# Cross attention with two levels of Strassen-Winograd products: VectorE's sums interleaved, three products moved to fresh PSUM banks, and product 5 in blocks in every batch but the first

## The chip, the cores and the metric

The kernel runs on one NeuronCore of one Trainium2 chip. The metric is the device time of one execution in microseconds (us); the time before is the median of three runs. A NeuronCore has four engines with instruction queues of their own that matter here: TensorE (PE in the profile), which multiplies matrices into PSUM banks, VectorE (DVE), ScalarE (ACT) and GpSimd (POOL). SyncE (SP) issues DMAs, and so does POOL. Each queue runs in order; engines wait for one another through semaphores.

## The reference

Eight batches of 512 channels by 1024 positions; everything is float32.

```python
B, C1, C2, N = (8, 512, 512, 1024)
q = jnp.einsum('bcn,dc->bnd', x1, Wq) + bq            # d = 64
k = jnp.einsum('bcn,dc->bdn', x2, Wk) + bk[:, None]
v = jnp.einsum('bcn,dc->bdn', x2, Wv) + bv[:, None]
attn = jax.nn.softmax(jnp.einsum('bnd,bdm->bnm', q, k), axis=2)
attn_out = jnp.einsum('bcm,bnm->bcn', v, attn)
return attn_out + x1
```

## The kernel before

**Stages.** The kernel reorders the output as Wv (x2 exp(scores)) / sum, plus bias and x1. Per batch there are four stages on PE: queries and keys (`project`, L173), scores (`scores`, L212), y = x2 times the exponentials e (512 by 1024, contracted over 1024 positions), and o = Wv times y. The scores are transposed, so that e has the position that is summed over on the partitions: `e[0]` and `e[1]` are the left and right half of the columns (h = 0, 1), each with two groups of four tiles of 128 positions.

**Seven products.** Both y and o are 2 by 2 block products done with seven multiplications in place of eight (Strassen's method in Winograd's form). `MULT` (L355) lists the seven: left operand, right operand, PSUM bank, and whether the product opens its bank. Left operands S1 to S4 and right operands T1 to T4 are sums of blocks. A "bank" here is a pair, `a0` and `a1` or `c0` and `c1`, one for each 128 rows. A result that belongs to several outputs stays in its bank while further products are added to it, with a copy taken in between: ScalarE copies bank a after product 1 (u1), after 6 (u6) and after 5 (u5). In the names of the code: y11 = product 2 + u1, U3 = (products 1 + 6) + product 7, y22 = U3 + product 5, y21 = U3 and product 4, and T3 of the next level, y22 - y12, is product 7 and product 3.

**Products in blocks.** A product can itself be done with seven smaller ones (`inner_product`, L438): 128 by 256 results, two tiles deep. `inner_left` (L412) forms four 128x256 sums of the left operand, `inner_right` (L421) one 128x1024 and two 128x512 sums of the right operand, all on VectorE. Two half banks from the pool "sc" (two buffers, used in turn), `chain` and `third`, take the partial results. `multiply_seeded` (L459) opens a fresh bank: ScalarE copies the chain into parts of it (after inner products 1, 6, 5 and 4), further inner products are added there, and `complete` (L483) adds the third part on VectorE. `multiply_onto` (L489) instead adds to a bank that is in use and evicts the chain to a tile d in SBUF, which VectorE then completes (L516) and adds. Before, `multiply_seeded` serves products 1, 2, 7 and 3, `multiply_onto` serves 4 (`multiply_4`, L520, with another sum at L524) and, in batches 1 to 5, product 5 (`multiply_5`, L526, with two sums at L531). In batch 0 and in batches 6 and 7 product 5 is plain (`first(5)`), as product 6 is everywhere.

**Order.** All instructions are put in order by hand (`manual_schedule`, L987); `period` (L764) writes one batch and, between its products, work of the next batches: `n` is the next batch, `nn` and `nnn` the ones after (None past the end), `five` is true in batches 1 to 5. `hooks` of a product are calls that are made after one of its inner products, such as an exponential on ScalarE. `scores_0` (L790) makes the scores of the next batch's half 0 (one of the four in bank c), the queries of the batch after, and the running maximum over tiles (`fold`, L242; `highest`, L254, has POOL reduce over partitions). `lower` (L290) subtracts the maximum, `exponential` (L295) follows. The scores of half 1 come after product 3, the third of them in bank a. The sums of the exponentials (`total`, L260; `invert`, L269; `spread`, L275) go through POOL, three small DMAs and VectorE; `scale_y` (L544) multiplies y by the inverse.

**Sums off VectorE.** T4 is made from a ScalarE copy and two accumulating DMAs on POOL's queue (`sum_t4`, L315), T3 by a ScalarE negation and two such DMAs (`sum_t3`, L326), in batches 1 to 6. In batch 7 VectorE makes T3 (`sum_e`, L337).

## Time and profile before

| | |
|---|---|
| median of three runs | 682.66 us |
| lowest and highest | 682.51 and 682.8 us |
| span of the profiled execution (its own run isn't among the three) | 680.8 us |
| PE busy | 672.1 us (99%) |
| VectorE busy | 615.2 us (90%) |
| ScalarE busy | 336.9 us (49%) |
| GpSimd busy | 218.5 us (32%) |
| chain that ended last: PE, VectorE, DMA | 84%, 6%, 5% |
| granted PE clock | 0.9 or more of full speed in every fortieth of the span |

The span runs from the first to the last instruction of the program on the core, so it leaves out what comes before and after. A row of a timeline has the start from the span's beginning, the length, engine, line, operation, written tile and read tiles, shape, the number of merged instructions, and in brackets the idle time before it with what ended it. A row of waits has the sum, the number and the longest. Matmuls overlap: the next one starts while the one before still shows as busy, so a product's price is the distance between two starts. In float32 each matmul of the code shows as two. The batches follow one another without a gap; the first product of a batch starts at 120.46 (batch 1), 204.21, 286.25, 368.24, 450.42, 532.41 and 608.83 us (batch 7).

### The profile page before, as it was taken

The numbers are of one execution on the slowest core, as the hardware profiler recorded it, in microseconds if no ns is written. First come the engines' busy times: TensorE is split into PE (matmuls) and PEld (weight loads), VectorE is DVE, ScalarE is ACT, GpSimd is POOL, SyncE is SP. The second block draws the span as 40 slices with busy tenths as digits, with TensorE's granted clock in tenths as the row PEclk, the third lists the DMA queues.
The fourth block names the chain that finished last, engine by engine and source line by source line (L and its number), as shares of the span: only waits on it lengthen the run. The fifth ranks groups of instructions, "written<-read, shape, count | busy, mean of one in ns | idle before, by whom it ended". The sixth has DMA issues, their size and how long they took to land.

```text
span 680.8 us, 7209 instructions
## 1 busy us (share of the span) xinstructions
PE 672.1 (99%) x2420; PEld 397.9 (58%) x2420; DVE 615.2 (90%) x763; ACT 336.9 (49%) x564; POOL 218.5 (32%) x182
## 2 busy tenths in 40 slices
PE   8999999999999999999999999999999999999997
PEld 5333554757547565566656576464854747556763
DVE  1999998899999999999999998999989979999884
ACT  2734266365554564544644637446475356553320
POOL 0124215251153502643125421344213451154100
PEclk9999999999999999999999999999999999999999
DMA  9656658967798759969499693996947985489503
GB/s 300 271 191 241 155 212 139 240 138 246 180 249 221 154 202 253 214 185 245 123 297 199 174 264 116 280 212 160 277 89 174 222 194 110 92 146 268 144 13 110
DMA packets 50772, 131.09 MB, mean 193 GB/s; under 512 B 5552, under 2 KB 7856, under 8 KB 50736
## 3 DMA queue, kind: packets, MB, share of 16 engines
q0 software_dynamic: 22464, 54.60, 44.7%
q1 hardware_dynamic: 27984, 75.64, 30.8%
q10 hardware_dynamic: 288, 0.39, 0.2%
q8 instruction: 19, 0.31, 0.2%
q14 instruction: 17, 0.14, 0.1%
HBM read 87.30 MB, written 16.81 MB: 153 GB/s over the span
## 4 chain that ended last, share of the span: by engine, by line
PE 84%; DVE 6%; DMA 5%; issue 2%; ACT 1%; SPq 1%; POOL 1%; DVEq 0%; POOLq 0%; ACTq 0%
PE ps_ya L380 11%; PE ps_oa L380 11%; PE ps_yc L442 8%; PE ps_oc L380 7%; PE ps_ya L442 6%; PE ps_s L228 5%; PE ps_o L400 4%; PE ps_o L380 4%; PE ps_k L181 3%; PE ps_q L181 3%; PE ps_i4chain L442 3%; PE ps_i3chain L442 3%; PE ps_i7chain L442 2%; PE ps_i1chain L442 2%; PE ps_i2chain L442 2%
## 5 line engine op out<-in xcount | busy, mean ns | idle before, releaser
L263 POOL PARTITION_ALL_REDUCE den<-sum x16 | 52.6, 3285 | 97.4 <-DVE few L271 60.3
L258 POOL PARTITION_ALL_REDUCE top<-max x16 | 37.6, 2352 | 126.3 <-DVE max L252 75.7
L380 PE MATMUL ps_ya<-eT,aS 128*128 128x512 f32 x176 | 77.5, 594 | 0.0
L293 DVE TENSOR_TENSOR e<-e,top 128x1024 f32<-128x1024 f32 x60 | 69.9, 1218 | 0.0
L620 POOL DMA_DIRECT2D sum<-e x21 | 32.1, 1530 | 108.7 <-ACT sum L625 42.0
L297 ACT ACTIVATE e<-e 128x1024 f32<-128x1024 f32 x60 | 61.8, 1058 | 4.7 <-DVE e L293 4.0
L380 PE MATMUL ps_oa<-yT,w_S 128*128 128x512 f32 x128 | 57.5, 592 | 0.0
L380 PE MATMUL ps_oc<-yT,w 128*128 128x512 f32 x128 | 57.4, 592 | 0.0
L380 PEld LDWEIGHTS ps_ya<-eT,aS 128*128 128x128 f32 x176 | 33.2, 190 | 40.1 <-issue 37.9
L237 ACT COPY e<-ps_s 128x1024 f32<-128x1024 f32 x46 | 45.6, 1032 | 9.0 <-PE ps_s L228 8.8
L228 PE MATMUL ps_s<-q,k 64*128 64x512 f32 x188 | 47.9, 608 | 0.9 <-ACT q L647 0.8
L380 PEld LDWEIGHTS ps_oa<-yT,w_S 128*128 128x128 f32 x128 | 24.3, 190 | 30.6 <-issue 30.6
L380 PEld LDWEIGHTS ps_oc<-yT,w 128*128 128x128 f32 x128 | 24.3, 190 | 30.6 <-issue 29.2
L248 DVE TENSOR_TENSOR max<-max,e 128x1024 f32<-128x1024 f32 x30 | 36.7, 1225 | 2.2
L391 ACT COPY uo<-ps_oa 128x512 f32<-128x512 f32 x32 | 18.7, 586 | 34.9 <-PE ps_oa L380 34.9
L391 ACT COPY uy<-ps_ya 128x512 f32<-128x512 f32 x24 | 13.9, 588 | 36.8 <-PE ps_ya L380 36.8
L228 PEld LDWEIGHTS ps_s<-q,k 64*128 64x128 f32 x188 | 17.1, 186 | 24.5 <-issue 18.0
L479 ACT COPY ps_ya<-ps_i1chain 128x256 f32<-128x256 f32 x28 | 10.0, 357 | 42.2 <-PE ps_i1chain L442 38.7
L547 DVE TENSOR_TENSOR y<-y,den 128x1024 f32<-128x1024 f32 x24 | 29.3, 1221 | 0.3
L418 DVE TENSOR_TENSOR aI<-a 128x256 f32<-128x256 f32 x58 | 29.4, 547 | 0.0
L380 PE MATMUL ps_oa<-y,w_S 128*128 128x512 f32 (+1 forms) x68 | 28.8, 567 | 0.0
L400 PE MATMUL ps_o<-y,w 128*128 128x512 f32 x64 | 28.8, 592 | 0.0
(202 smaller groups left out, 1539.0 us busy)
## 6 DMA issues: line engine op xcount, KB each, us to landing
x_in_x_dram<-in_x_dram SPq DMA_DIRECT2D x60, 512.0 KB, 7.6
a<-in_x2T_dram SPq DMA_DIRECT2D x32, 512.0 KB, 10.1
sum<-e POOLq DMA_DIRECT2D x21, 512.0 KB, 10.1
aS<-in_x2T_dram POOLq DMA_DIRECT2D x14, 512.0 KB, 8.9
uo<-in_x_dram POOLq DMA_DIRECT2D x14, 512.0 KB, 9.9
r<-in_x_dram POOLq DMA_DIRECT2D x14, 512.0 KB, 12.2
out_dram<-r SPq DMA_DIRECT2D x14, 512.0 KB, 6.5
eT<-eT POOLq DMA_DIRECT2D x14, 512.0 KB, 10.1
```

Of the source, the lines that this page charges most:

```text
L181: nc.tensor.matmul(ps[r, :], w_sb[:, c, :], s.x[:, c, ts(h, H)], start=(c == 0), stop=(c == CT - 1),)
L228: nc.tensor.matmul(ps[g], s.k[r, ts(i, P)], s.q[r, ts(h, H)], start=True, stop=True)
L237: nc.scalar.copy(e[:, :, i, :], whole)
L248: nc.vector.tensor_tensor(f, e[:, :, 0, :] if i == 1 else f, e[:, :, i, :], op)
L258: nc.gpsimd.partition_all_reduce(s.top[h], s.mx[h][:, 0, :], P, ReduceOp.max)
L263: nc.gpsimd.partition_all_reduce(s.den[h], s.mx[h][:, 0, :], P, ReduceOp.add)
L293: nc.vector.tensor_tensor(e, e, top, ALU.subtract)
L297: nc.scalar.activation(e, e, AF.Exp)
L380: nc.tensor.matmul(ps[:, n], left[ka][:, k, ts(j, P)], right[kb][:, k, n], start=opens and k == 0, stop=i in (2, 3, 4) and k == n_k - 1, s ...
L391: nc.scalar.copy(s.tmp[i][:, j, :], ps)
L400: nc.tensor.matmul(ps, w["11"][:, k, ts(j, P)], s.y["11"][:, k, :], start=k == 0, stop=False, skip_group_check=True)
L442: nc.tensor.matmul(ps, s.inner[i][ka][:, k, :], s.inner[i, "t"][kb][:, k, :], start=opens and k == 0, stop=z in (2, 3, 4) and k == MH // 2 ...
```

## The change

- `weave` takes several streams of VectorE sums and issues them in turn, one from each. `left_stream` and `right_stream` are `inner_left` and `inner_right` as streams, `folds` and `lowers` are streams of these steps. Woven are: the folds of the sums of half 1 with product 7's left sums, the left and right sums of products 5 and 4, product 7's right sums with product 3's left ones, product 3's right sums with one lowering, and the next batch's right sums for product 1 with its left sums for product 2. From batch 1 on T1 is made for both pairs of tiles before T2.
- Product 5 is made by `multiply_seeded` in a fresh bank a in batches 1 to 7, so also in blocks in batches 6 and 7.
- Product 3 goes to a fresh bank c, product 4 to a fresh bank c (batch 7: bank a), from batch 1 on. ScalarE's copies of product 7 move ahead of product 3 and behind its second inner product. `join_67` adds u6 and that copy once; y22 is bank a + the sum, y21 bank c (batch 7: a) + the sum. `multiply_seeded` takes its second half bank only after the second inner product.
- Batch 7: T3 comes from ScalarE and DMAs as in the other batches, the total of half 1 and the inverse of half 0 are made later, and the sum T1 of y moves behind y21.

Batch 0 keeps its order and its product 4.

```diff
 
+    def folds(s, h, kind, op):
+
+        for i in range(1, MH):
+            fold(s, h, i, kind, op)
+            yield
+
     def fold_halves(s, h, op):
...
 
+    def lowers(s, h, of, to):
+        for i in range(of, to):
+            lower(s, h, i)
+            yield
+
     def exponential(s, h, i):
...
 
-    def sum_e(s, *ks, of=(0, 2)):
-        for i in of:
-            part = {n: v[:, i : i + 2, :] for n, v in s.t.items()}
-            for k in ks:
-                right_sums(part, k)
+    def sum_e(s, *ks):
+        order = [(k, i) for i in (0, 2) for k in ks]
+        for k, i in order if s.b == 0 else sorted(order):
+            right_sums({n: v[:, i : i + 2, :] for n, v in s.t.items()}, k)
 
...
     )
-    def inner_left(s, i, x, tag):
+    def weave(*streams):
+
+        streams = list(streams)
+        while streams:
+            for stream in list(streams):
+                if next(stream, "end") == "end":
+                    streams.remove(stream)
+
+    def left_stream(s, i, x, tag):
 
...
         sums = sb.tile([P, 4, MH // 2, P], F32, tag=tag, name=f"aI{i}_{s.b}")
+        s.inner[i] = v
         for z, (k, x, y, op) in enumerate(LEFT):
...
             nc.vector.tensor_tensor(v[k], v[x], v[y], op)
-        s.inner[i] = v
+            yield
 
-    def inner_right(s, i, x, *tags):
+    def inner_left(s, i, x, tag):
+        weave(left_stream(s, i, x, tag))
 
-        v = {
-            f"{q + 1}{r + 1}": x[:, ts(q, MH // 2), ts(r, H // 2)] for q in range(2) for r in range(2)
-        }
+    def right_stream(s, i, x, *tags):
+
+        half = x.shape[1] // 2
+        v = {f"{q + 1}{r + 1}": x[:, ts(q, half), ts(r, H // 2)] for q in range(2) for r in range(2)}
         last = 4 // len(tags)
-        shape = [P, last, MH // 2, H // 2]
+        shape = [P, last, half, H // 2]
         sums = [sb.tile(shape, F32, tag=t, name=f"eI{i}{t}_{s.b}") for t in tags]
...
         )
+        s.inner[i, "t"] = v | {"T1": both[:, 0], "T3": both[:, 1], "T2": t2, "T4": t4}
+        yield
         nc.vector.tensor_tensor(t2, both[:, 0], v["22"], ALU.subtract)
+        yield
         nc.vector.tensor_tensor(t4, v["21"], t2, ALU.add)
-        s.inner[i, "t"] = v | {"T1": both[:, 0], "T3": both[:, 1], "T2": t2, "T4": t4}
+        yield
+
+    def inner_right(s, i, x, *tags):
+        weave(right_stream(s, i, x, *tags))
 
...
 
-    def multiply_seeded(s, i, v_tag, hooks={}):
+    def multiply_seeded(s, i, v_tag, hooks={}, bank=None):
 
-        bank = MULT[i][2]
-        b0, b1 = (
-            ps_a.tile([P, H], F32, tag=f"{bank}{j}", name=f"ps_y{bank}{j}_{s.b}_{i}") for j in range(2)
-        )
-        s.bank[bank, 0], s.bank[bank, 1] = b0, b1
+        bank = bank or MULT[i][2]
+
+        def fresh(j):
+            s.bank[bank, j] = ps = ps_a.tile(
+                [P, H], F32, tag=f"{bank}{j}", name=f"ps_y{bank}{j}_{s.b}_{i}"
+            )
+            return ps
+
+        b0 = fresh(0)
         chain, third = inner_parts(s, i)
         v = sb.tile([P, 2, H], F32, tag=v_tag, name=f"v{i}_{s.b}")[:, 0, left]
-        for z, ps, opens, out, of in (
-            (1, chain, True, b0[:, left], chain),
-            (7, third, True, v, third),
-            (6, chain, False, b1[:, left], chain),
-            (2, b0[:, left], False, None, None),
-            (5, chain, False, b0[:, right], chain),
-            (4, b1[:, left], False, b1[:, right], chain),
-            (3, b0[:, right], False, None, None),
-        ):
+        def step(z, ps, opens, out=None, of=None):
             inner_product(s, i, z, ps, opens)
...
 
+        step(1, chain, True, b0[:, left], chain)
+        step(7, third, True, v, third)
+        b1 = fresh(1)
+        step(6, chain, False, b1[:, left], chain)
+        step(2, b0[:, left], False)
+        step(5, chain, False, b0[:, right], chain)
+        step(4, b1[:, left], False, b1[:, right], chain)
+        step(3, b0[:, right], False)
+
         def complete():
...
 
-        d, complete = multiply_onto(s, 4, "u5" if s.b < B - 1 else "a21", "r", hooks)
+        d, complete = multiply_onto(s, 4, "u5", "r", hooks)
         complete()
...
 
-    def multiply_5(s, hooks):
-
-        d, complete = multiply_onto(s, 5, "u5", "r", hooks)
-        complete()
-        for j in range(2):
-            nc.vector.tensor_tensor(d[:, j, :], s.bank["a", j], d[:, j, :], ALU.add)
-        s.tmp[5] = d
+    def join_67(s):
+        nc.vector.tensor_tensor(s.tmp[6], s.tmp[6], s.tmp[7], ALU.add)
 
...
         for j in range(2):
-            nc.vector.tensor_tensor(y[:, j, :], s.bank["a", j], s.tmp[7][:, j, :], ALU.add)
+            nc.vector.tensor_tensor(
+                y[:, j, :], s.bank["c" if s.b else "a", j], s.tmp[7][:, j, :], ALU.add
+            )
 
...
         bank, add = RESULT[k]
+        if s.b and k == "22" or s.b == B - 1 and k == "21":
+            bank, add = "a", 6
         s.y[k] = y = sb.tile([P, 2, H], F32, tag=f"y{k}", name=f"y{k}_{s.b}")
...
             complete_1()
-            for i in range(1, MH):
-                fold(s, 1, i, "sum", ALU.add)
-            total(s, 1)
-            invert(s, 0)
+            sums_5 = left_stream(s, 5, s.a["S1"], "i2"), right_stream(s, 5, s.t["T1"], "y21", "u1")
+            if n:
+                weave(folds(s, 1, "sum", ALU.add), left_stream(s, 7, s.a["S3"], "yT4"))
+                total(s, 1)
+                invert(s, 0)
+            else:
+                weave(folds(s, 1, "sum", ALU.add), left_stream(s, 7, s.a["S3"], "yT4"))
+                weave(*sums_5)
             complete_2 = multiply_seeded(
...
             )
-            if n:
-                sum_t3(s, 0)
-                sum_t3(s, 2)
+            sum_t3(s, 0)
+            sum_t3(s, 2)
+            if n is None:
+                total(s, 1)
             complete_2()
             evict_y(s, "11")
-            if n is None:
-                sum_e(s, "T3")
             sum_t4(s)
             first(6)
-            inner_left(s, 7, s.a["S3"], "yT4")
-            if five:
-                inner_left(s, 5, s.a["S1"], "i2")
-                inner_right(s, 5, s.t["T1"], "y21", "u1")
-            sum_a(s, "S4")
             if n:
+                weave(*sums_5)
+            if n:
+                sum_a(s, "S4")
                 evict_q = scores_0()
-            spread(s, 0)
-            shares(s, 1)
-            inner_right(s, 7, s.t["T3"], "yT1", "yT2")
-            inner_left(s, 3, s.a["S4"], "aI3")
-            if five:
-                multiply_5(s, {6: evict_q})
+                spread(s, 0)
+                shares(s, 1)
+            if n:
+                weave(right_stream(s, 7, s.t["T3"], "yT1", "yT2"), left_stream(s, 3, s.a["S4"], "aI3"))
             else:
-                first(5)
-            inner_right(s, 3, s.t["22"], "eT1")
+                sum_a(s, "S4")
+                weave(right_stream(s, 7, s.t["T3"], "yT1", "yT2"), left_stream(s, 3, s.a["S4"], "aI3"))
+                invert(s, 0)
+                spread(s, 0)
+            complete_5 = multiply_seeded(
+                s, 5, "r", {6: evict_q} if five else {}, "a"
+            )
+            complete_5()
+            if n is None:
+                shares(s, 1)
             if n:
-                lower(n, 0, 0)
+                weave(right_stream(s, 3, s.t["22"], "eT1"), lowers(n, 0, 0, 1))
+            else:
+                inner_right(s, 3, s.t["22"], "eT1")
             complete_7 = multiply_seeded(s, 7, "y12")
             complete_7()
-            evict_y(s, "22")
+            hooks = {7: lambda: copy_7(s, 1)}
             if n:
-                for i in range(1, MH):
-                    lower(n, 0, i)
-            else:
+                hooks |= {6: lambda: exponential(n, 0, 0), 4: lambda: exponential(n, 0, 1)}
+            copy_7(s, 0)
+            if n:
+                lower(n, 0, 1)
+            complete_3 = multiply_seeded(s, 3, "r", hooks, "c")
+            if n is None:
                 inner_left(s, 4, s.a["22"], "a12")
+            join_67(s)
+            evict_y(s, "22")
+            if n is None:
                 inner_right(s, 4, s.t["T4"], "eT2")
-
-            hooks = {2: lambda: copy_7(s, 0), 5: lambda: copy_7(s, 1)}
             if n:
-                hooks |= {6: lambda: exponential(n, 0, 0), 4: lambda: exponential(n, 0, 1)}
-            complete_3 = multiply_seeded(s, 3, "r", hooks)
+                for i in range(2, MH):
+                    lower(n, 0, i)
             complete_3()
...
         if late and n:
-            inner_left(s, 4, s.a["22"], "a12")
-            inner_right(s, 4, s.t["T4"], "eT2")
+            weave(left_stream(s, 4, s.a["22"], "a12"), right_stream(s, 4, s.t["T4"], "eT2"))
         if late:
...
         sum_y(s, "T2")
-        sum_y(s, "T1")
+        if n:
+            sum_y(s, "T1")
         if s.b == 0:
...
                 hooks[7] = first_sum
-        multiply_4(s, hooks)
+        if s.b == 0:
+            multiply_4(s, hooks)
+        else:
+            complete_4 = multiply_seeded(s, 4, "r", hooks, "c" if n else "a")
+            complete_4()
         if late and n:
...
         evict_y(s, "21")
+        if n is None:
+            sum_y(s, "T1")
         scale_y(s, "21")
...
         if n:
-            inner_right(n, 1, n.e[0][:, 0], "yT1", "yT2")
-            inner_left(n, 2, n.a["12"], "aS4")
+            weave(
+                right_stream(n, 1, n.e[0][:, 0], "yT1", "yT2"), left_stream(n, 2, n.a["12"], "aS4")
+            )
             inner_right(n, 2, n.e[0][:, 1], "eT4")
```

6 lines of the change are left out of this document (3 added, 3 removed).

## The prediction

> **What bounds the kernel now.** I read the page's spans first, then the busy time batch by batch (each stretch runs from one batch's first product to the next one's).
>
> ```profile
> span 680.8 us, 7209 instructions
> PE 672.1 (99%) x2420; PEld 397.9 (58%) x2420; DVE 615.2 (90%) x763; ACT 336.9 (49%) x564; POOL 218.5 (32%) x182
> core 0: us, PE busy (x) PEld busy (x) DVE busy (x) ACT busy (x) POOL busy (x), PEclk, DMA share, GB/s
> 286.25:368.24 81.99, 81.99 (x306) 50.52 (x304) 77.88 (x99) 43.72 (x74) 28.96 (x24) 1.00 0.83 208
> 120.46:204.21 83.75, 82.86 (x306) 50.71 (x305) 77.71 (x99) 44.21 (x74) 28.93 (x24) 1.00 0.87 210
> 532.41:608.83 76.42, 76.13 (x261) 46.05 (x260) 70.70 (x88) 41.49 (x68) 28.71 (x24) 1.00 0.69 147
> 608.83:680.80 71.97, 68.16 (x233) 43.87 (x231) 56.00 (x74) 18.71 (x41) 11.83 (x11) 1.00 0.50 138
> ```
>
> Batch 3 (286.25) is 81.99 us long and PE is busy in all of it, at a granted clock of 1.00. So in the steady batches VectorE is close behind (77.88) but sets nothing: a microsecond saved on it there is worth nothing, and a new wait of PE costs its full length. Batch 1 is 1.76 us longer than batch 3 for the same instructions. PE's waits say why:
>
> ```profile
> PE ps_sa L228 <- DVE yT L542: 0.9, 1, 0.9
> PE ps_i4third L442 <- ACT e L237: 0.3, 1, 0.3
> 161.40 0.69 DVE L485 TENSOR_TENSOR ps_yc<-ps_yc,v 128x512 f32<-128x512 f32 x1
> 167.20 1.28 DVE L542 TENSOR_TENSOR yT<-ps_ya,uy 128x512 f32<-128x512 f32 x2
> 167.94 1.29 PE L228 MATMUL ps_sa<-q,k 64*128 64x512 f32 x3 [0.89 <-DVE yT L542]
> 170.44 3.65 PE L181 MATMUL ps_k<-x_in_x_dram,wqk_sb 128*64 128x512 f32 x16
> ```
>
> Scores of the next batch want bank a, and VectorE reads product 3 out of it late (until 168.48). In all only three things can be won: batch 1's 1.76 us, PE work in batches 6 and 7, and the small wait in batch 6.
>
> **Part 1, product 5 in blocks.** The next fence has a block product (batch 3, begun by the row at 312.51, followed by product 7 at 318.66) and the plain one (batch 6).
>
> ```profile
> 312.51 1.13 PE L442 MATMUL ps_i5chain<-eT,aS 128*128 128x256 f32 x4
> 318.66 0.59 PE L442 MATMUL ps_i7chain<-e,a 128*128 128x256 f32 x2
> 555.09 7.13 PE L380 MATMUL ps_ya<-eT,aS 128*128 128x512 f32 x16
> 562.06 0.81 PE L442 MATMUL ps_i7chain<-e,a 128*128 128x256 f32 x3
> ```
>
> Blocks take 318.66-312.51 = 6.15 us, the plain form 562.06-555.09 = 6.97. That is 0.82 us of PE in each of batches 6 and 7, 1.64 together. For it VectorE gets seven more sums per batch. One 128x1024 sum lasts 1.22 and overlaps an independent next one by 0.08:
>
> ```profile
> 291.46 1.23 DVE L306 TENSOR_TENSOR eT<-eT,e 128x1024 f32<-128x1024 f32 x1
> 292.60 1.22 DVE L306 TENSOR_TENSOR eT<-e,e 128x1024 f32<-128x1024 f32 x1
> 293.85 1.23 DVE L306 TENSOR_TENSOR eT<-eT,e 128x1024 f32<-128x1024 f32 x1
> 654.07 0.69 DVE L516 TENSOR_TENSOR d<-d,v 128x512 f32<-128x512 f32 x1
> 629.26 0.75 DVE L418 TENSOR_TENSOR aI<-a 128x256 f32<-128x256 f32 x2
> ```
>
> The sum at 292.60 starts 0.09 before the one at 291.46 ends, since it doesn't read its result; the one at 293.85 reads its predecessor's result and starts 0.03 after it. So an independent sum costs 1.14, 0.60 or 0.34 us by size, and a dependent neighbour 0.12 more. The seven sums cost 1.14+2x0.60+4x0.34 = 3.7 us. In batch 6 that time is free: VectorE waits for copied scores just then, over 3 us. The price if the cover were gone is a few tenths, product 5's second step being due 0.97 after 555.09.
>
> ```profile
> DVE max L248 <- ACT e L235: 3.3, 1, 3.3
> ```
>
> **Part 2, the weave.** It parts 23 dependent neighbours per batch, 23x0.12 = 2.8 us of VectorE. [...]
>
> **Part 3, fresh banks.** Per batch VectorE loses L531 twice (2x0.60) and L524 (1.23) and gets the joined sum (1.22), net 1.2 us less; L516 becomes L485, of the same size. ScalarE's copies stay five to a product. Bank a is now read last by y22's eviction rather than by T3's. In batch 1 VectorE reaches product 7's completion (161.40 before) about 3 us sooner: 1.2 for L531, 1.8 for 15 parted neighbours. It can't run before ScalarE's copy that it adds to, which ends at 158.61:
>
> ```profile
> 158.25 0.36 ACT L479 COPY ps_yc<-ps_i7chain 128x256 f32<-128x256 f32 x1 [0.51 <-PE ps_yc L442]
> ```
>
>  so completion at 159.3, the second copy of 7 at 161.7 (behind product 3's second copy), the joined sum at 163.0, y22 at 164.2. PE wants bank a at 166.9. All 1.76 us go; the bound on the other side is none of them.
>
> The move has a price on ScalarE. Product 4 was evicted to SBUF twice right after its fifth step; now its last copy comes after the sixth step, behind the exponential hooked to the fifth:
>
> ```profile
> 342.68 0.65 ACT L451 COPY d<-ps_i4chain 128x256 f32<-128x256 f32 x2 [0.40 <-PE ps_i4chain L442]
> 343.21 1.07 ACT L297 ACTIVATE e<-e 128x1024 f32<-128x1024 f32 x1
> 344.21 2.31 PE L400 MATMUL ps_o<-y,w 128*128 128x512 f32 x5
> 579.29 1.13 PE L442 MATMUL ps_i4third<-eI4eT,aI 128*128 128x256 f32 x4 [0.29 <-ACT e L237]
> 580.26 1.03 PE L442 MATMUL ps_i4chain<-eI4eT,aI 128*128 128x256 f32 x4
> ```
>
> One copy (0.37) from 342.68, the exponential from about 342.95 to 344.01, then the last copy to about 344.26. L400's first tile takes the buffer of that chain (two "sc" buffers, in turn), so its matmuls, at 344.21 now, wait until about 344.31. A stall also costs a refill: behind the wait at 579.29 the next step comes after 0.97 instead of 0.86. So 0.10+0.10 = 0.2 us in each of batches 1 to 5, 1.0 us in all. Bounds: nothing, if the copy is 0.1 sooner; 0.35 each (1.75), if the copy runs as long as the longest idle that PE shows behind ScalarE, 0.29, and a little more. Queued behind that copy on ScalarE are only the negation of a (needed a stage later) and L404.
>
> In the same batches the other deadlines hold. Joined sum, y22, two lowers and product 3's completion end T3 about 2 us later than before (334.3 for 332.4), product 4's sums are then due at 339.0 and ready at 336.0. The weave delays the totals of half 1 by 0.9 us on VectorE, and behind them POOL's reduction, its two small DMAs and the four accumulating DMAs of T3 and T4; R7 reads T3 around 313 and PE needs it at 319.5.
>
> **Part 4, batches 6 and 7.** In batch 6 everything from product 7 on moves up 0.82. Product 4 follows the scores at once (no keys), its sums are ready at 578.1, and ScalarE frees the buffer with the row at 578.18, moved up to end at 578.4; so the wait of 0.29 stays, and L400 starts about 0.8 sooner. In batch 7 VectorE becomes the bound. It starts after a transfer (second row):
>
> ```profile
> 578.18 1.06 ACT L237 COPY e<-ps_s 128x1024 f32<-128x1024 f32 x1
> 612.04 0.69 DVE L252 TENSOR_TENSOR sum<-sum 128x512 f32<-128x512 f32 x1 [1.10 <-DMA sum<-e]
> 613.97 2.18 DVE L306 TENSOR_TENSOR eT<-e,e 128x1024 f32<-128x1024 f32 x1
> 633.30 0.18 DVE L271 RECIPROCAL few<-few 128x4 f32<-128x4 f32 x1 [1.24 <-DMA few<-den]
> 654.70 0.57 ACT L404 COPY ps_oa<-ps_o 128x512 f32<-128x512 f32 x1 [2.80 <-PE ps_o L400]
> 656.22 3.60 PE L380 MATMUL ps_oa<-yT,w_S 128*128 128x512 f32 x8
> ```
>
> That transfer's issue waits for batch 6's maxima, which VectorE now ends about 1.1 us sooner (L524 and parted sums); I let 613.97 become 612.9 (bounds: unmoved, and 1.1). Up to y21's first half VectorE then has 16 sums of 1.14, one of 2.1, 22 of 0.60, 16 of 0.34, two reciprocals (0.2), eight dependent neighbours (1.0), 0.4 for a sum slowed beside POOL's reduction (as the 2.18 at 613.97 is) and 0.9 of waits (the reciprocal for few, whose reduction now starts 3.5 us later; the joined sum for product 7's copy): 18.2+2.1+13.2+5.4+0.2+1.0+0.4+0.9 = 41.4, so 654.3 to 654.6. New is who waits for it: product 4 lies in bank a here, and L404 writes bank a for product 6 of the output. L404 goes from 654.5 to 655.1, and PE's 656.22 becomes about 655.15; with the refill of 0.1 the end gains 0.95 instead of 1.64. Bounds: 1.9 (PE alone, with batch 6's wait gone), and minus 0.3 with the start unmoved.
>
> **Sum**: -1.76 (batch 1) +1.0 (product 4's last copy) -0.95 (batches 6 and 7, at the end) = -1.7, from a span of 680.8 that stands 1.9 under the median of 682.66; that part is untouched. Forecast 680.9 us. A measurement tells 0.2% (1.4 us) from no change, so this is just on the faster side.
>
> **Rivals.**
> 1. Nothing new stalls: product 4's copy is in time and batch 7 keeps up. -1.76-1.64-0.3 = -3.7: 679.0. For it: the margin missed is 0.1 us. Against: the exponential's 1.07 stands in the queue. 0.17.
> 2. Batch 1's wait doesn't go but moves to the chain completion, copy of 7, joined sum, y22. Then 682.66+1.0-0.95 = 682.7. Against it: 2.7 us of slack by the rows. 0.09.
> 3. Parting sums saves nothing. Batch 1 still catches up through L531, but batch 7's 14 parted neighbours (1.7 us) come back, the end loses 0.75 instead of winning 0.95: 682.66-1.76+1.0+0.75 = 682.7. [...] 0.06.
> 4. Batch 7 gives both blocks' savings back and no more: 682.66-1.76+1.0 = 681.9. 0.03 beside the forecast's own spread.
> 5. Slower: in batch 7 T3 is no longer summed by VectorE (L306 twice, below) but by two accumulating DMAs, beside the loads of x. The next fence has that sum, then these DMAs' time to landing in batches 1 to 6 (of T3 first, of T4 behind it).
>
> ```profile
> 626.57 2.77 DVE L306 TENSOR_TENSOR e<-e 128x1024 f32<-128x1024 f32 x2
> e<-e POOLq DMA_DIRECT2D x12, 512.0 KB, 5.8
> DMA to landing us min/median/max: 4.7/5.8/8.2
> eT<-eT POOLq DMA_DIRECT2D x14, 512.0 KB, 10.1
> DMA to landing us min/median/max: 5.9/10.1/13.9
> ```
>
> The second is issued about 624.3 (third fold, then the negation). R7 wants it at 631.7 and PE at 632.7, so 5.8 to 8.2 is in time. At the 13.9 of the other row R7 starts 6.5 late, 0.9 of it in waits that are there anyway: the end comes 5.6 later, 682.66-1.76+1.0-0.95+5.6 = 686.6. It decides from a landing of about 11.4. Against it: here nothing else is ahead of it on POOL's queue. 0.09.
> 6. Product 4's last copy frees its buffer only with the instruction behind it on ScalarE (another 1.06): 1.1 more in five batches, 680.9+5.5 = 686.4. Against it: the wait at 579.29 ended 0.05 after its copy. 0.06.
>
> **How the numbers follow.** Forecast 0.50, of which 0.39 lie more than 0.2% under 682.66 (under 681.3) and 0.11 above. Faster: 0.39+0.17 = 0.56. Same: 0.11+0.09+0.06+0.03 = 0.29. Slower: 0.09+0.06 = 0.15. The forecast's own range is 679.9 to 682.1, from the bounds of part 3's copy (-1.0 to +0.75) and of part 4 (-0.95 to +1.25), one at a time. From rival 1's 679.0 to 683.8, past rivals 2 to 4, some 0.2 is left out, nearly all of it rivals 5 and 6.
>
> **What would show it.** Right: batch 1 as long as batch 3 and no PE wait on scores in bank a; product 5 at 6.15 us in batches 6 and 7; a PE wait of L400 on ScalarE of 0.1 to 0.2 us in batches 1 to 5, so steady batches of 82.2; L404 in the last batch waiting for VectorE's y21, and PE's next product for L404; VectorE's idle in steady batches grown from 4.1 to about 8 us. Wrong: steady batches of 81.99 (rival 1) or over 83 (rival 6); batch 1 still over 83 (2); dependent neighbours' time unchanged (3); PE idle at product 7 of batch 7 on T3's DMA (5). A wait of PE in every batch that isn't named here would break the forecast most, since each 0.3 us counts five to six times.

## The result, and the profile after

The changed kernel takes **684.83 us** (median of six executions, 683.85 to 686.8) against 682.34 us for the kernel before on the same chip (six executions, 681.43 to 682.8): a ratio of 1.0043, 95% interval 1.003 to 1.0056. It is slower, by 2.5 us (0.4%), where 680.9 was forecast.

First the page of the profiled execution, which took 686.8 us (the slowest of the six): its span, two busy lines and, of the forty slices, the granted PE clock.

```profile
span 684.7 us, 7307 instructions
...
PE 673.8 (98%) x2444; PEld 403.5 (59%) x2444; DVE 603.5 (88%) x767; ACT 341.4 (50%) x572; POOL 217.7 (32%) x184
...
PEclk9999999999999999999999999999999999999899
```

VectorE is busy for 11.7 us less than before, as was meant. But PE's clock has a slice below 0.9, which the page before did not have. The stretches by batch, in the columns shown before (here batches 1, 3, 6 and 7):

```profile
120.08:202.07 81.99, 81.99 (x306) 50.45 (x304) 74.02 (x97) 44.21 (x74) 28.02 (x24) 1.00 0.88 216
284.06:366.05 81.99, 81.99 (x305) 50.37 (x304) 75.01 (x97) 44.02 (x74) 28.96 (x24) 1.00 0.83 209
530.23:606.48 76.25, 75.46 (x274) 48.02 (x273) 73.73 (x95) 42.24 (x71) 28.91 (x24) 1.00 0.70 147
606.48:684.70 78.22, 70.65 (x245) 47.94 (x243) 56.46 (x80) 21.35 (x46) 13.32 (x13) 0.96 0.53 139
```

Batch 1 has lost its 1.76 us and is now as long as batch 3. Batch 6 gained only 0.17. Batch 7 went from 71.97 to 78.22: **6.25 us were lost there**. PE's waits after:

```profile
PE ps_i7third L469 <- DVE eI7yT L452: 3.3, 1, 3.3
...
PE ps_oa L390 <- ACT ps_oa L414: 0.5, 1, 0.5
PE ps_i5chain L469 <- ACT e L237: 0.5, 1, 0.5
...
PE ps_i4third L469 <- ACT e L237: 0.3, 1, 0.3
```

The wait for scores in bank a (`ps_sa`, 0.9) is gone. The first row is new: the second inner product of product 7 of batch 7 waits for VectorE's right sums. VectorE's own timeline there (start, length, line, tiles, and in brackets the idle time before it):

```profile
628.96 1.71 DVE L108 SCALAR_TENSOR_TENSOR aS<-a,aS 128x1024 f32<-128x1024 f32 x1
634.39 1.23 DVE L452 TENSOR_TENSOR eI7yT<-e 128x1024 f32<-128x1024 f32 x1 [3.71 <-DMA e<-e]
```

VectorE was ready at 628.96+1.71 = 630.67 and idled 3.71 us for T3, that is for the second of the two accumulating DMAs of L341. They were issued at 620.62 and 623.56. The view of that line in this stretch, and the chain that ended last (start, length, what), in which it stands now, say how long they took:

```profile
L341 POOL DMA_DIRECT2D e<-e x2: 837/853/869, 620.6 to 623.6; - x2
...
DMA to landing us min/median/max: 9.0/9.9/10.7
```

```profile
623.56 10.71 DMA e<-e
```

10.71 us to landing, where batches 1 to 6 of the kernel before showed 4.7 to 8.2 for these DMAs. What PE made of it:

```profile
631.47 1.03 PE L469 MATMUL ps_i7chain<-e,a 128*128 128x256 f32 x4
635.76 2.05 PE L469 MATMUL ps_i7third<-eI7yT,aI 128*128 128x256 f32 x4 [3.26 <-DVE eI7yT L452]
637.60 1.91 PE L469 MATMUL ps_i7chain<-eI7yT,aI 128*128 128x256 f32 x4
639.30 1.91 PE L469 MATMUL ps_yc<-e,a 128*128 128x256 f32 x4
641.01 1.26 PE L469 MATMUL ps_i7chain<-eI7yT,aI 128*128 128x256 f32 x4
642.11 1.03 PE L469 MATMUL ps_yc<-eI7yT,a 128*128 128x256 f32 x4
...
643.83 1.03 PE L469 MATMUL ps_i3chain<-e,aS 128*128 128x256 f32 x4
```

Product 7 took 643.83-631.47 = 12.36 us; undisturbed it takes 6.05 (before: 634.65 to 640.70). The difference of 6.31 has two parts. The idle time is 635.76-631.47-0.86 = 3.43, since a step undisturbed takes 0.86. The rest, 2.9, comes after the wait: the next steps stand 1.84, 1.70, 1.71 and 1.10 apart instead of 0.86, with nobody waited for. The stretch behind the wait says why (the clock is third from the end):

```profile
636.00:642.00 6.00, 6.00 (x16) 4.80 (x17) 5.50 (x11) 0.73 (x2) 1.67 (x3) 0.54 0.54 105
```

From 636 to 642 us PE ran at a mean granted clock of 0.54. It had fallen during the wait: it is 1.00 from 631 to 634.5 and 0.55 in the next stretch, so it fell about 2.1 us after PE's last matmul had ended (631.47+1.03 = 632.50).

```profile
634.50:636.00 1.50, 0.24 (x1) 0.27 (x2) 1.50 (x3) 0.00 (x0) 0.00 (x0) 0.55 1.07 213
```

This second part is not in every execution: over the span the six had clocks of 0.995 (the profiled one), 0.997, 1.0, 1.0, 0.998 and 0.998, and the two at 1.0 took 684.31 and 683.85 us.

### The profile page after: what moved, and what is told of

Its sections match the earlier page's. It is cut to its first block, busy times and chain, and to the rows that moved or that the text cites. A ratio compares the mean times of both kernels' runs of the same rounds, so it can differ in the third digit from the quotient of the medians.

```text
span 684.7 us, 7307 instructions
## 1 busy us (share of the span) xinstructions
PE 673.8 (98%) x2444; PEld 403.5 (59%) x2444; DVE 603.5 (88%) x767; ACT 341.4 (50%) x572; POOL 217.7 (32%) x184
## 4 chain that ended last, share of the span: by engine, by line
PE 84%; DMA 7%; DVE 4%; issue 2%; ACT 2%; SPq 1%; POOL 0%; DVEq 0%; ACTq 0%; POOLq 0%
PE ps_oa L390 11%; PE ps_yc L469 10%; PE ps_ya L390 9%; PE ps_oc L390 7%; PE ps_s L228 5%; PE ps_ya L469 5%; PE ps_q L181 4%; PE ps_o L390 4%; PE ps_k L181 3%; PE ps_o L410 3%; PE ps_i3chain L469 3%; PE ps_i4chain L469 3%; PE ps_i7chain L469 3%; PE ps_i5chain L469 2%; PE ps_i1chain L469 2%; PE ps_i2chain L469 2%
## 5 line engine op out<-in xcount | busy, mean ns | idle before, releaser
L264 POOL PARTITION_ALL_REDUCE top<-max x16 | 35.1, 2194 | 113.4 <-DVE max L258 70.6
L390 PE MATMUL ps_ya<-eT,aS 128*128 128x512 f32 x144 | 63.5, 593 | 0.0
L390 PEld LDWEIGHTS ps_ya<-eT,aS 128*128 128x128 f32 x144 | 27.2, 190 | 32.1 <-issue 29.8
L517 DVE TENSOR_TENSOR ps_yc<-ps_yc,v 128x512 f32<-128x512 f32 x27 | 18.7, 692 | 12.3 <-ACT ps_yc L502 12.3
L410 PE MATMUL ps_o<-y,w 128*128 128x512 f32 x64 | 28.8, 592 | 0.0
L390 PE MATMUL ps_o<-y,w 128*128 128x512 f32 x64 | 28.8, 592 | 0.0
```

The source lines that it names most:

```text
L264: nc.gpsimd.partition_all_reduce(s.top[h], s.mx[h][:, 0, :], P, ReduceOp.max)
L390: nc.tensor.matmul(ps[:, n], left[ka][:, k, ts(j, P)], right[kb][:, k, n], start=opens and k == 0, stop=i in (2, 3, 4) and k == n_k - 1, s ...
L410: nc.tensor.matmul(ps, w["11"][:, k, ts(j, P)], s.y["11"][:, k, :], start=k == 0, stop=False, skip_group_check=True)
```

## The experiments

**Theory A**: T3's DMAs land late since the four loads of x of batch 7 (512 KB each, on SP's queue) run beside them; a low clock behind the wait adds to it. The code has these loads at the batch's start (606.48), but in SP's queue they stand behind three output DMAs, the last of them issued at 619.49. So they are issued from 619.96 on, next to T3's at 620.62 and 623.56:

```profile
619.96 2.90 SPq L137 DMA_DIRECT2D x_in_x_dram<-in_x_dram  x4
```

**Rivals**, with the letters of the expectations below: B, T3's DMAs are as slow by themselves; C, VectorE is late there whatever the DMAs do, by the seven sums of product 5; D, the slow steps behind the wait come from transfers under way, not from idle time. A last one, E, is looked at in experiments 5 to 8: what was lost lies in the weave, the blocks or the last copy of product 4. Experiment 9's expectation has an A and a B of its own. All kernels below are the changed kernel with one edit, except where the text says so. Profiled executions differ by up to 1.2 us in when batch 1 begins (119.60 to 120.77 in these runs), so the sizes are taken from the length of batches and from medians, not from spans.

**1. The loads of x a batch earlier.** (`e1_x_early`)

```diff
-        if n is None:
-            load_x(s, x1)
...
                 evict_q = scores_0()
+                if nn is None:
+                    load_x(n, x1)
```

> The changed kernel, with the loads of x1 for the last batch issued in batch 6, behind the scores of the last batch's half 0, in place of the start of batch 7. Theory A (the loss is T3's second accumulating DMA in batch 7, slowed by these four loads): that DMA lands 6 to 7 us after its issue in place of 10.7, R7 starts when VectorE is free (about 19 us after S4's predecessor, no wait over 1 us), PE's wait of 3.3 us before product 7's second step is gone, the granted clock stays at 1.00; the span falls by 6.3 (3.4 of wait, 2.9 of low clock) to about 678.4, the time to about 680.3, ratio about 0.997. Theory B (that DMA is slow by itself, 16 accumulating transfers behind one another): it lands after 10 us again, the time stays at 684 to 685.

Measured: 680.67 us (679.69 to 681.18, ten executions) against 682.19, ratio 0.9974, interval 0.9965 to 0.9982. The DMAs of L341 in batch 7, VectorE's first right sum of product 7, and batches 6 and 7:

```profile
DMA to landing us min/median/max: 4.8/4.9/5.0
```

```profile
631.05 1.21 DVE L452 TENSOR_TENSOR eI7yT<-e 128x1024 f32<-128x1024 f32 x1
```

```profile
530.92:607.16 76.24, 75.45 (x274) 48.01 (x272) 73.01 (x95) 42.23 (x71) 27.95 (x24) 1.00 0.75 174
607.16:679.00 71.84, 67.60 (x245) 46.03 (x243) 56.26 (x80) 21.35 (x46) 13.33 (x13) 0.99 0.50 123
```

The row at 631.05 has no bracket: nobody waits for T3. The landing halves, the wait and the low clock go, and the kernel is faster than before. Of the change's own median this one place costs 684.83-680.67 = 4.2 us. Theory A stands; B falls by the landing of 4.9 us, C by the row at 631.05.

**2. Half of the loads earlier.** (`e8_half_early`) Two of the four tiles move as in experiment 1, two stay at the start of batch 7 (`load_x` called with the tiles 0 and 1, then with 2 and 3).

> The changed kernel with two of the four loads of x1 for the last batch in batch 6 and two at the start of batch 7. If the loads slow T3's second accumulating DMA in proportion, it lands 7 to 8.5 us after its issue (4.9 with none beside it, 10.7 with four), that is at about 631.5: a wait of PE at product 7 of 0 to 1 us, no loss of clock, time 680.7 to 681.7. If the loads matter only by standing ahead of it in the queue at that moment, one of two values: as e1 or as the change.

Measured: 681.98 us (680.9 to 684.83, twelve executions), ratio 0.9997, interval 0.9988 to 1.0006. Landing and PE's wait:

```profile
DMA to landing us min/median/max: 8.5/8.7/8.9
```

```profile
PE ps_i7third L470 <- DVE eI7yT L453: 1.4, 1, 1.4
```

The second DMA lands after 8.5 us, the upper end of the expectation; PE's wait and the time are a little above it (1 us and 681.7 at most). None, two and four loads beside them give median landings of 4.9, 8.7 and 9.9 us, and PE waits of 0, 1.4 and 3.3: two loads already cost most of the landing. How full the DMA engines are in the same 16 us, first in the kernel before, then after, with half the loads and with none (the last two columns are the share of the DMA engines and GB/s):

```profile
620.00:636.00 16.00, 16.00 (x45) 8.06 (x44) 14.52 (x21) 5.64 (x10) 7.25 (x7) 1.00 0.97 286
```

```profile
620.00:636.00 16.00, 12.74 (x47) 8.47 (x46) 12.25 (x20) 6.49 (x12) 7.27 (x6) 0.96 1.02 288
```

```profile
620.00:636.00 16.00, 14.59 (x55) 9.94 (x55) 14.42 (x24) 7.14 (x14) 7.28 (x6) 1.00 0.96 227
```

```profile
620.00:636.00 16.00, 16.00 (x61) 11.38 (x60) 15.93 (x29) 7.67 (x14) 7.85 (x7) 1.00 0.71 166
```

The first of these rows is the one that should have been read before the forecast. **The kernel before already had the 16 DMA engines 0.97 busy in that stretch**, without T3's two DMAs in it. The average over batch 7, 0.50, hid it.

**3. T3 on VectorE again** (`e2_t3_vector`) in batch 7, behind y11, as in the kernel before; all else stays changed.

```diff
-            sum_t3(s, 0)
-            sum_t3(s, 2)
+            if n:
+                sum_t3(s, 0)
+                sum_t3(s, 2)
...
             evict_y(s, "11")
+            if n is None:
+                sum_e(s, "T3")
```

> The changed kernel, with T3 of the last batch summed by VectorE again (two sums behind y11), the loads of x1 where the change has them. Theory A: no DMA is waited for, but VectorE reaches R7 2.3 us later than it could (about 633.0) and PE waits about 1.9 us at product 7; with the clock kept the end comes 1.5 + 2.9 sooner, time about 680.5; if 1.9 us of idle is enough for the clock to drop, about 683. Theory C (the seven sums of product 5 are what makes batch 7 late, not T3's DMAs): PE's wait at product 7 stays over 3 us and the time at 684 or more.

Measured: 682.61 us (twelve executions, 681.26 to 685.13 and one of 707.22 with a clock of 0.949 over the span), ratio 1.0006, interval 0.9997 to 1.0015. VectorE's sum and the first right sum of product 7, then PE:

```profile
629.56 2.83 DVE L317 TENSOR_TENSOR e<-e 128x1024 f32<-128x1024 f32 x2
...
633.46 1.21 DVE L452 TENSOR_TENSOR eI7yT<-e 128x1024 f32<-128x1024 f32 x1
```

```profile
634.81 1.10 PE L469 MATMUL ps_i7third<-eI7yT,aI 128*128 128x256 f32 x4 [1.88 <-DVE eI7yT L452]
635.75 1.10 PE L469 MATMUL ps_i7chain<-eI7yT,aI 128*128 128x256 f32 x4
```

VectorE waits for no DMA in this stretch and isn't idle, and PE still waits 1.9. Batch 7 is 681.0-606.91 = 74.09 us long, 2.25 more than in experiment 1. So with product 5 in blocks VectorE has no room for T3 in batch 7: taking it off VectorE was right, and only the place of the loads was wrong. The time is neither the 680.5 nor the 683 of the expectation; the first took 2.9 us of low clock off the median, which holds less of it (the changed kernel's executions at full clock took 684.31 and 683.85).

In this execution the step behind a wait of 1.88 takes 0.94, not 1.84: the clock stayed. That isn't so in each. Two others of the twelve, apart from the longest, have a clock of 0.997 and 0.998 over the span and took 684.12 and 685.13 us; one in experiment 2 (0.998, 684.83) and one in experiment 5 (0.997, 683.3) are like them. These four weren't profiled, so how long PE waited in them isn't known. The kernels without a PE wait over 1.1 us (experiments 1, 4 and 6 to 9) have no execution under 0.999 among 53.

**4. PE kept busy during the wait.** (`e3_pe_filled`) Four matmuls of 128x512 into a half bank that nobody reads stand ahead of the second inner product of product 7 in batch 7; the loads stay where the change has them.

```diff
+        if i == 7 and s.b == B - 1:
+            for _ in range(4):
+                nc.tensor.matmul(
+                    s.spare, spare["w"], s.t["T1"][:, 0, :], start=True, stop=True, skip_group_check=True
+                )
         step(7, third, True, v, third)
...
```

> The changed kernel, with four more matmuls (128 by 512, about 3.4 us, into an unused half of a PSUM tile, on the warm-up weights) ahead of product 7's second step in the last batch, where PE waited. Theory A with the clock as a cause of its own: the wait for R7 is still there and is filled, the granted clock stays at 1.00 in the 6 us behind it, the steps of product 7 take 0.86 us again, the span falls by about 2.9 to 681.8 and the time to about 682 to 684. Theory D (the slow steps behind the wait come from the transfers that are under way, not from the idle time): the steps stay at 1.7 to 1.9 us, span 684.7.

Measured: 684.53 us (684.28 to 684.99, five executions), ratio 1.0033, interval 1.002 to 1.0046.

```profile
632.20 3.60 PE L510 MATMUL ps_i7third<-eT,warm 128*128 128x512 f32 x8
636.42 1.13 PE L469 MATMUL ps_i7third<-eI7yT,aI 128*128 128x256 f32 x4 [0.63 <-DVE eI7yT L452]
...
641.85 1.03 PE L469 MATMUL ps_i3chain<-e,aS 128*128 128x256 f32 x4
```

```profile
636.00:642.00 6.00, 5.58 (x25) 4.74 (x26) 5.90 (x13) 1.44 (x4) 1.11 (x2) 1.00 0.56 110
```

T3 is as late (it lands after 11.1 us, and the second step starts at 636.42), but from there to product 3 it is 641.85-636.42 = 5.43 us, where the changed kernel's profile has 643.83-635.76 = 8.07. In the 6 us from 636 the clock is 1.00 here and 0.54 there, at a DMA share of 0.56 and 0.54; and all five executions have 0.999 or 1.0 over the span, where four of the changed kernel's six have less. So here it was the idle time of PE that lowered the clock, not the load on the DMA engines, and theory D falls. The time is hardly under the changed kernel's median and above the 682 to 684 expected: the fill removes the second loss only from the executions that have it, and the wait itself stays.

**5. Experiment 1 without the weave** (`e5_no_weave`): the streams one after another, and T1 and T2 in the old order.

```diff
-        streams = list(streams)
-        while streams:
-            for stream in list(streams):
-                if next(stream, "end") == "end":
-                    streams.remove(stream)
+        for stream in streams:
+            for _ in stream:
+                pass
...
-        for k, i in order if s.b == 0 else sorted(order):
+        for k, i in order:
```

> e1 (loads of x1 early) without the weave: each pair of streams one after the other, and T1 and T2 in the old order. If parting dependent sums is worth 0.12 us each only where VectorE is late, the steady batches stay at 81.99, batch 1 too (the fresh banks alone take 1.2 us of VectorE off, and bank a is read sooner), and only batch 7 grows, by up to 1.7 us at the wait of product 6 of the output (0.5 in e1) and at product 7: time 0.5 to 1.7 over e1's 680.7. If the weave is worth nothing anywhere: as e1. If it is what keeps the steady batches: 81.99 grows in each.

Measured: 682.17 us (681.46 to 683.3, eleven executions), ratio 1.0003, interval 0.9994 to 1.0011. A wait of PE, and batches 1, 2 and 6:

```profile
PE ps_i4third L467 <- DVE eI4eT L450: 1.6, 1, 1.6
```

```profile
119.81:201.99 82.18, 82.18 (x305) 51.22 (x304) 75.88 (x97) 44.21 (x74) 28.03 (x24) 1.00 0.88 216
201.99:283.98 81.99, 81.99 (x305) 50.37 (x304) 76.76 (x97) 44.14 (x74) 28.05 (x24) 1.00 0.84 209
530.16:607.69 77.53, 75.41 (x274) 48.09 (x273) 75.09 (x97) 41.90 (x71) 27.99 (x24) 1.00 0.77 173
```

The weave is worth 682.17-680.67 = 1.5 us, and most of it is in batch 6 (77.53 against 76.24), where the expectation had nothing: product 4's right sums now come 1.6 late. There it is the order that counts more than the parting. Without the weave all four left sums stand ahead of the first right sum, which starts at 576.81, 1.58 behind the first left one (575.23); woven, it starts 0.33 behind it (576.10 and 575.77), and of the right sums PE's second step waits for that one alone. All seven sums together take 4.17 us in a row and 3.68 woven. Batch 1 keeps nearly all of its gain without the weave. VectorE is busy for 76.76 us in a steady batch (batch 2), 1.8 more than with the weave (74.99 in batch 2 of experiment 1), for the same 97 instructions.

**6. The kernel before with the weave alone** (`e6_weave_only`) (the same streams, no fresh banks, no new blocks, T3 of batch 7 on VectorE).

> The kernel before with the weave alone: old banks, old product 4 and 5, batch 7's products and DMAs as before. VectorE should reach product 7's completion in batch 1 about 1.8 us sooner and T3's second half about 166.7 for 168.5, where PE wants bank a at 166.9: PE's wait for bank a in batch 1 goes or shrinks to under 0.3, the time falls by 1.3 to 1.8 to about 680.6. If only the fresh banks release bank a in time, the wait stays above 0.5 and the time above 681.5.

Measured: 680.68 us (680.39 to 680.95, eleven executions) against 682.31, ratio 0.9978, interval 0.9969 to 0.9986. Batch 1:

```profile
120.08:202.41 82.33, 82.33 (x305) 50.80 (x304) 75.32 (x99) 44.00 (x74) 27.98 (x24) 1.00 0.88 214
```

The weave alone takes 83.75-82.33 = 1.42 us from batch 1, as expected, and PE's wait for scores in bank a is gone from its list. The fresh banks without the weave (experiment 5) take 83.75-82.18 = 1.57. They are two remedies for one wait; either is nearly enough, and together they can't win it twice.

**7. Experiment 1 with product 5 plain** (`e7_plain_5`) in batches 6 and 7, as before, and without its sums there.

> e1 with product 5 plain in batches 6 and 7 (into its fresh bank a), without the seven sums for it. By PE's work alone it costs 1.64 us more than e1: 682.3. By the waits that the block form brings in e1 (0.5 and a refill at its first step in batch 6, where no queries stand between the scores and it; 0.5 at product 6 of the output in batch 7, where VectorE is late) most of that comes back: 0.3 to 0.8 over e1, 681.0 to 681.5.

Measured: 681.57 us (680.59 to 682.0, eleven executions), ratio 0.999, interval 0.9981 to 0.9998. Its batches 6 and 7 begin at 530.18 and 606.62 and the span ends at 679.3, so they are 76.44 and 72.68 us long, against 76.24 and 71.84 in experiment 1: the blocks are worth 0.84 in batch 7, as forecast, but 0.20 in batch 6. The wait for scores (`ps_i5chain`) is gone here; the one of product 6 of the output stays, at 0.5.

**8. Product 4's last copy later** (`e4_late_copy`) in batches 1 to 5: experiment 1 with one more ScalarE instruction of 1.05 us ahead of that copy (a copy of e onto itself).

```diff
-            hooks = {6: lambda: add_exponential(2), 5: lambda: exponential(n, 0, 3)}
+            def last_exponential():
+                exponential(n, 0, 3)
+                if nn:
+                    e3 = n.e[0][:, :, 3, :]
+                    nc.scalar.copy(e3, e3)
+
+            hooks = {6: lambda: add_exponential(2), 5: last_exponential}
```

> e1 (loads of x1 early) with one more ScalarE copy of 1.06 us, an exponential's tile onto itself, behind the exponential hooked to product 4's fifth step in batches 1 to 5, so that product 4's last copy comes 1.06 us later. If the output's first tile takes the buffer of product 4's chain, as the prediction had it, L410's first matmuls wait about 1.0 us in each of five batches and the steady batches grow from 81.99 to about 83.0, time 5 us over e1. If it takes the other buffer (that of the third part), nothing of PE moves: steady batches of 81.99, time as e1.

Measured: 680.38 us (679.98 to 681.4, ten executions), ratio 0.9977, interval 0.9968 to 0.9986: as experiment 1. ScalarE, then PE, in batch 3:

```profile
341.38 1.05 ACT L971 COPY e<-e 128x1024 f32<-128x1024 f32 x1
342.33 0.37 ACT L502 COPY ps_yc<-ps_i4chain 128x256 f32<-128x256 f32 x1
```

```profile
341.54 2.74 PE L410 MATMUL ps_o<-y,w 128*128 128x512 f32 x6
```

PE's next product starts 0.79 us before that copy does, and doesn't wait for it; the steady batches are still 81.99 long. The copy is not on the path.

**9. y21 ahead of y22's scaling** (`e9_y21_first`) in batch 7, with experiment 1's loads.

```diff
-            scale_y(s, "11", "T3", "22")
+            scale_y(s, "11", "T3")
+            if n:
+                scale_y(s, "22")
...
-        if n is None:
-            sum_y(s, "T1")
         scale_y(s, "21")
+        if n is None:
+            scale_y(s, "22")
+            sum_y(s, "T1")
```

> The changed kernel with the early loads of x (as in e1_x_early, 680.67 us), and in the last batch y22's scaling by VectorE moved from ahead of y21's scaling to behind it, so that y21 is ready about 1.2 us earlier if VectorE's own queue is what holds it. Theory A (VectorE's queue is what product 6 of the output waits for in the last batch): the wait of 0.5 us at the first product into ps_oa goes, the last batch is about 0.5 us shorter, time about 680.1 us. Rival B (ScalarE's copies of the last sums are what holds y21, VectorE has slack there): the wait of ps_oa stays between 0.4 and 0.6, time as e1_x_early, about 680.7 us. A third way: y22, now later, makes another product of the last batch wait; then a new row of a wait of PE on ps_oa or a neighbour, and a time at or above 680.7.

Measured: **679.92 us** (678.98 to 680.38, six executions) against 681.84, ratio 0.9967, interval 0.9954 to 0.9979, the fastest of all. The first product into `ps_oa` in experiment 1, then here:

```profile
650.28 3.60 PE L410 MATMUL ps_o<-y,w 128*128 128x512 f32 x8
654.39 3.70 PE L390 MATMUL ps_oa<-yT,w_S 128*128 128x512 f32 x8 [0.51 <-ACT ps_oa L414]
```

```profile
650.25 3.60 PE L410 MATMUL ps_o<-y,w 128*128 128x512 f32 x8
653.68 3.60 PE L390 MATMUL ps_oa<-yT,w_S 128*128 128x512 f32 x8
```

4.11 us become 3.43, and no row of a wait takes its place: VectorE's own queue held y21, not ScalarE's copies. The edit also moves the sum T1 behind y21's scaling, but T1 stood behind y21's first half already (654.20 and 653.00 in experiment 1), so it is y22's scaling that held it. That this version beats experiment 1 is read from these rows; the two intervals overlap, and they come from different chips.

## Why the prediction was wrong

| term | forecast, us | measured, us | from |
|---|---|---|---|
| batch 1 | -1.76 | -1.76 | stretches of before and after |
| product 4's last copy, batches 1 to 5 | +1.0 | 0 | steady batches still 81.99; experiment 8 |
| batch 6 | -0.82 | -0.17 | stretches |
| batch 7 without rival 5 | -0.13 | -0.13 | 71.97 and 71.84 (experiment 1) |
| late T3 in batch 7 | rival 5, at 0.09 | +4.2 in the median, +6.4 in the profiled execution | experiment 1 |
| time outside the span | 0 ("that part is untouched") | +0.3 | 1.8 in the kernel before and in experiments 3 and 6, 2.1 in the changed kernel and all others |

The third and fourth rows part the forecast's 0.95 for the end as its text does: 0.82 moves up in batch 6, and the rest is batch 7. The last row goes with T3's two DMAs in batch 7: experiment 3, which differs from the changed kernel only in making this T3 on VectorE, has 1.8. Why they lengthen what lies outside the span no run shows. With the medians' +4.2 the measured column adds up to +2.4, and +2.5 was measured.

**The step that failed** is the one on rival 5: "R7 wants it at 631.7 and PE at 632.7, so 5.8 to 8.2 is in time", and against the rival "here nothing else is ahead of it on POOL's queue". The rival names the loads of x beside these DMAs, but against it only POOL's queue was looked at. The landing of 5.8 to 8.2 was read from batches 1 to 6 and carried to a stretch whose own DMA share was not. There it was 0.97 before the DMAs came, and they took 10.7. Loads on another queue were enough for that: T3's DMAs, on POOL's queue, had median landings of 4.9, 8.7 and 9.9 us beside none, two and four loads on SP's.

The rival's arithmetic was also too lenient. It had VectorE ready 631.7-624.3 = 7.4 us after the second DMA's issue, and it was ready after 630.67-623.56 = 7.1. It counted 0.9 us of the lateness as waits that are there anyway, but product 6 of the output still waited its 0.5. And it had no term for the clock. With a landing of 10.71 it gives 624.3+10.71-631.7-0.9 = 2.4 us of loss, 683.3 on top of the forecast; the fastest of the changed kernel's executions, at full clock, took 683.85.

**The clock** was in no term. Behind 3.26 us of idle time it fell to a mean of 0.54 for 6 us, which cost 2.9; in the profiled executions behind 1.88 (experiment 3) and 1.41 (experiment 2) it stayed, and with the gap filled it stayed too (experiment 4). The changed kernel's executions differ in their clock, 0.995 to 1.0 over the span. In the profiled one it fell about 2.1 us into the idle time. That is little more than the waits of 1.88 and 1.41, and three executions of experiments 2 and 3 have a clock of 0.997 or 0.998; so a wait of under 3 us isn't shown to be safe.

**Part 1, the blocks.** The price was right: in batch 6 product 5 takes 559.69-553.49 = 6.20 us, for 6.15 forecast. What was missed is who waits: product 5's chain takes one of the "sc" buffers that scores hold, which the plain form doesn't.

```profile
553.49 1.13 PE L469 MATMUL ps_i5chain<-eT,aS 128*128 128x256 f32 x4 [0.50 <-ACT e L237]
...
559.69 1.03 PE L469 MATMUL ps_i7chain<-e,a 128*128 128x256 f32 x4
```

So batch 6 gives back 0.5 and a refill of its 0.82. In batch 7, where no scores come ahead, the blocks win 0.84 (experiment 7).

**Part 2, the weave.** That parting dependent sums saves VectorE time was right, the size too large: 23 parted neighbours were costed at 2.8 us of VectorE per batch, its busy time differs by 1.8 (experiment 5; busy time leaves out the short gaps between dependent instructions, 0.03 us ahead of the row at 293.85 that the prediction shows), and its idle time in a steady batch grew from 4.1 to 81.99-75.01 = 7.0, not to 8. Rival 3 would have the weave save nothing; experiment 6 shows 1.6 us of the kernel's time (682.31 to 680.68), most of it in batch 1, where VectorE completes product 7 sooner. Experiment 5's 1.5 us say less on this point, since in batch 6 the order of the sums alone moves the first right sum by 1.58-0.33 = 1.25. The place was wrong too: the forecast had product 4's sums of batch 6 in time and the weave paying in batch 7, and without it batch 6 is 1.3 longer and batch 7 only 0.3 (679.8-607.69 = 72.11).

**Part 3, the fresh banks.** Batch 1 came out to the hundredth. The text adds up the banks (1.2 us of VectorE) and the parted sums (1.8); either is nearly enough, 1.57 by the banks and 1.42 by the weave (experiments 5 and 6). The price of product 4's last copy was a mistake: L410's first tile doesn't wait for the chain's buffer. In the profile after, too, its matmuls start at 342.02 while the copy, 0.38 us from 341.72, still runs. The pool has two buffers, and the chain's is still being read; so the tile must lie in the other one, the third part's, as experiment 8's expectation had it. That is inferred from the code's two buffers; no view names them.

**Part 4.** y21 as the bound of product 6 of the output was right: a wait of about 0.4 was forecast (PE at 655.15, the tiles before it ending at 652.78-1.64+3.60 = 654.74), 0.5 is there, and experiment 9 shows that it is VectorE's queue. Experiment 9 comes to rival 1's batches but for batch 6's two waits, with a batch 7 of 71.13 us, 0.84 less than before, and yet gains 1.9 us (681.84 to 679.92), not 3.7. What the rest is, beyond those waits and the 0.3 outside the span, no run shows.

So the mechanism that decided was on the list, with its place, and held to be unlikely for want of one row. Without it experiment 1's 680.67 stands beside the forecast's 680.9, but that is luck: +1.0 too much at product 4 is cancelled by 0.65 too little lost in batch 6 and 0.3 outside the span.

## What to carry to other kernels

Before a sum is moved from an engine to a DMA, read the DMA share of the very stretch in which it will run, all queues together, not the mean of the stage and not the landing times of other stages. A wait of PE can have a second price, the low clock behind it, and the clock fell about 2.1 us into the profiled one: four of six executions paid it with a profiled wait of 3.3 us, few with profiled waits of 1.4 to 1.9, and the same kernel pays it in one execution and not in the next, so read the clock of every execution. When a change holds several remedies, run each alone: here reordering VectorE's sums alone gave as much (680.68) as all of it with the loads moved (680.67), and the blocks paid only where nothing else held their buffers. And reordering has two effects that a run should part: which sum comes first, and which neighbours depend on each other.

## What was not expected of the hardware

- The granted clock fell about 2.1 us into one idle time of 3.26 us and was at a mean of 0.54 in the 6 us behind it; in the profiled executions it didn't fall in waits of 1.88 and 1.41.
- Two 512 KB accumulating DMAs landed in 4.9 us (median) without, and in 9.0 to 10.7 with, four 512 KB loads from another queue beside them, and the loads were slowed as well: their median went from 7.1 to 10.7 us (kernel before and after, the 28 us from 612):

```profile
x_in_x_dram<-in_x_dram SPq DMA_DIRECT2D x4, 512.0 KB, 7.1
```

```profile
x_in_x_dram<-in_x_dram SPq DMA_DIRECT2D x4, 512.0 KB, 10.7
```
